# Four-head layer of a graph attention stack: the first group of three neighbours added by VectorE, head by head, in place of TensorE

## The chip, the core and the metric

One core of a Trainium2 chip. The kernel is a single launch that computes four layers; its time is device microseconds of that core, given as the median of several runs. TensorE (PE) does matrix products into PSUM; VectorE (DVE), ScalarE (ACT) and GpSimd (POOL) work along the columns of 128 partitions; SyncE (SP) and POOL issue the DMAs. POOL's indirect DMAs gather table rows by index.

## The reference

Four layers of graph attention with a residual. x is 3327 x 512, adj a 3327 x 3327 matrix of 0 and 1 with some 16 ones in a row. A layer, cut to what matters (layer 1, the second, with four heads of 128 columns):

```
h  = max(layernorm(x), 0)
Wh = (h @ W).reshape(n, 4, 128)
sl, sr = (Wh * a_l).sum(-1), (Wh * a_r).sum(-1)
e  = leaky_relu(sl[i] + sr[j], 0.2), -inf where adj[i, j] == 0
x  = x + elu(sum_j softmax_j(e)[i, j, head] * Wh[j, head])
```

The layers have 8, 4, 1 and 8 heads. What the change touches is the last line's sum over j: a weighted sum of the neighbours' rows, with one weight per neighbour and head, divided at the end by the sum of the weights.

## The kernel before, in words

A first stage (up to about 310 us) turns adj into lists of neighbours, sorted by length. The 26 tiles of 128 rows each then have a fixed number of neighbours, `CAPS`: tile 0 has 36, tile 1 has 25, tile 2 has 23, down to 11 for tile 25. A layer works through its tiles from 25 downward. In layer 1 tiles 25 to 1 go by lists (class `Tile`) and tile 0 is computed densely beside them (class `Several`, spread over the layer's steps).

A list tile is cut into groups of four neighbours (`GROUP`), and a group is a step. `fetch` brings the group's table rows into one of seven buffers g (L865 the tile's own row by SP, L834 the neighbours by POOL's gathers). `scored` computes the group's weights: z on VectorE (L887, L889), then the exponential on ScalarE (L890) into `wt`, a slice of a PSUM tile pw. `group` multiplies the rows by the weights and sums them:

- with one head (layer 2) VectorE does all of it: one `scalar_tensor_tensor` per neighbour over 512 columns, accumulating in PSUM (L909, L911);
- with more heads VectorE multiplies each neighbour's 512 columns by the weights, broadcast over each head's columns (L918). The tile's first neighbour goes straight into the PSUM bank `po`, the others into a buffer m (three of them, four neighbours each), and TensorE adds every m row to the bank by a matmul with the identity (L923). In fp32 each such matmul is two MATMULs in the profile.

When a tile's last group is done, `divisors` (L929 to L931) and, two steps on, `means` (L941) divide the bank; then come the ELU (`bent`, L947 and L949 on ScalarE; L955 on VectorE), the residual (L961), the layer norm for the next layer (L969, L972 on ScalarE; L977, L438, L440 on VectorE), four transposes and sixteen projection MATMULs (`project`, L468), and the scaled row (`rows`, L475 on ScalarE), which SP writes to the next layer's table (L995).

The dense tile 0 takes in every few steps: two loads by SP (L1250, L1251), weights on ScalarE (L1261, L1262, L1267), scaled features (L1278, L1279), the mask on VectorE (L1283) and products on TensorE (L1301).

The order on all engines but SP is written out by hand (`manual_schedule`): each engine runs its instructions in the order in which the program issues them. Step s issues its fetches (7 ahead), the pieces put at "first" (the dense tile's mask and products, transposes), the scores of step s + 1, the pieces put at "scored", the group of step s, and the pieces at "last" (divisors, means, the residual, the projection).

Of the kernel before, what the change touches and what calls it, by code (L numbers as in the profile page):

```python
# [15 lines left out]
OP = mybir.AluOpType  # L16
AX = mybir.AxisListType

P = 128
# [3 lines left out]
HEADS = [8, 4, 1, 8]  # L23
# [11 lines left out]
ROW = 528  # L35
# [488 lines left out]
def tile_gat_stack(ctx: ExitStack, tc: tile.TileContext, x, adj, adjT, ws, avs, out):  # L524
# [266 lines left out]
    with cond.Else():  # L791
        tile_gat_lists(tc, x, adj, ws, avs, out, ident, half, slots, L, low, spare, tabx, tabs)
# [3 lines left out]
def tile_gat_lists(ctx: ExitStack, tc: tile.TileContext, x, adj, ws, avs, out, ident, half, slots, L, low, spare, tabx, tabs):  # L796
# [7 lines left out]
    nc = tc.nc  # L804
    NP, F = x.shape
# [39 lines left out]
    class Tile:  # L845
# [51 lines left out]
        def group(self, i):  # L897


            H, K, wt = HEADS[self.l], CAPS[self.t], self.wt  # L900
            D = F // H
            k0, n, g = self.groups[i]
            if H == 1:
                for q in range(n):
                    v = g[:, q, :].rearrange("p (s m) -> p s m", s=2)[:, :, :F // 2]
                    acc = self.po.rearrange("p (s m) -> p s m", s=2)
                    w = wt[:, k0 + q, 0:1]
                    if k0 + q == 0:
                        nc.vector.tensor_scalar(acc, v, w, None, OP.mult)  # L909
                    else:  # L910
                        nc.vector.scalar_tensor_tensor(acc, v, w, acc, OP.mult, OP.add)  # L911
                return
            m = pools["m"].tile([P, GROUP, F], F32, name="m")
            for q in range(n):
                v = g[:, q, :].rearrange("p (s m) -> p s m", s=2)[:, :, :F // 2]

                out_ = self.po if k0 + q == 0 else m[:, q, :]
                nc.vector.tensor_tensor(out_.rearrange("p (s h d) -> p s h d", s=2, d=D),  # L918
                                        v.rearrange("p s (h d) -> p s h d", d=D),
                                        wt[:, k0 + q, :H].rearrange("p (s h) -> p s h", s=2)  # L920
                                        .unsqueeze(3).to_broadcast([P, 2, H // 2, D]), OP.mult)
            for q in range(k0 == 0, n):
                nc.tensor.matmul(self.po, ident, m[:, q, :], start=False, stop=(k0 + q == K - 1),  # L923
                                 skip_group_check=True)

        def divisors(self):
            H, K = HEADS[self.l], CAPS[self.t]
            den = self.den = small.tile([P, 8], F32, name="den")
            nc.vector.tensor_reduce(den[:, :H], self.wt[:, :K, :H].rearrange("p k h -> p h k"), AX.X, OP.add)  # L929
            nc.vector.tensor_scalar_max(den[:, :H], den[:, :H], TINY)  # L930
            nc.vector.reciprocal(den[:, :H], den[:, :H])  # L931
# [420 lines left out]
    for l in range(NL):  # L1352
# [3 lines left out]
        with ExitStack() as c2:  # L1356
# [44 lines left out]
            for s in range(-1, at_end):  # L1401
# [10 lines left out]
                if 0 <= s < len(steps):  # L1412
                    tl, i = steps[s]
# [55 lines left out]
```

## Time and profile before

| | |
|---|---|
| runs of the kernel before | 3008.34 us median of 3 (2991.2 to 3010.58) |
| span of the profiled execution, first to last instruction | 2971.7 us (its own time around the span is not given) |
| busy: TensorE, VectorE, ScalarE, POOL | 2211.9, 1923.1, 934.6, 1731.4 us |
| the four layers in the span | 315 to 1106, 1106 to 1850, 1850 to 2311, 2311 to 2972 us |
| L923, sums on TensorE, the whole kernel | 2414 MATMULs; 812 of them in layer 1 |
| L918, products on VectorE | 1207 into m and 74 into the bank; 406 and 25 of them in layer 1 |

Busy times of TensorE are modelled and overlap: a MATMUL of 512 fp32 columns lasts 0.59 us in the records and the next starts 0.43 us after it. The clock column of the windows view is TensorE's mean granted clock; TensorE's clock is seen to halve now and then, and MATMULs then start 0.85 us apart.

### The profile page before, as it was taken

To read this page: it belongs to the slowest core of one execution; us is meant where nothing else is said; L and a number is where in the kernel's file an instruction comes from. 1 tells how busy PE (TensorE), PEld (TensorE's weight loads), DVE (VectorE), ACT (ScalarE), POOL (GpSimd) and SP (SyncE) were. 2 spreads that over 40 slices of the span, in tenths; PEclk is the share of its full clock that TensorE was granted. 3 is DMA by queue.
4 is the path that set the end of the run, shared out by engine and by line. 5 is a ranking of instruction groups with operands and counts; after the bars stand their busy time and mean duration, and the time that the engine had idled before them with its cause. 6 is when DMAs were issued, how large, how long until landed. Compare 5 with 4: busy or idle time off the path is not lost.

```text
span 2971.7 us, 27155 instructions
## 1 busy us (share of the span) xinstructions
PE 2211.9 (74%) x7082; PEld 1246.1 (42%) x7082; DVE 1923.1 (65%) x4968; ACT 934.6 (31%) x2502; POOL 1731.4 (58%) x1717
## 2 busy tenths in 40 slices
PE   4777677776777764767777877588696688878887
PEld 2564233343433332434444444244354454545443
DVE  7987666655565533656665665598888366666665
ACT  5872122322221111322222322244333333323330
POOL 7885455565566635544556562676664556555653
PEclk9988888888898887988888898799898898989888
DMA  6885576786676756755667673787785566656663
GB/s 230 325 291 161 165 228 200 211 254 207 195 225 197 199 130 200 200 157 174 187 190 210 179 209 92 234 255 240 241 246 153 168 193 204 185 170 198 195 189 111
DMA packets 260731, 594.21 MB, mean 200 GB/s; under 512 B 103699, under 2 KB 121107, under 8 KB 256214
## 3 DMA queue, kind: packets, MB, share of 16 engines
q0 software_dynamic: 124368, 432.13, 49.8%
q1 hardware_dynamic: 132454, 153.45, 16.4%
q10 hardware_dynamic: 3744, 6.82, 0.7%
q8 instruction: 57, 0.93, 0.1%
q14 instruction: 108, 0.88, 0.1%
HBM read 542.60 MB, written 49.65 MB: 199 GB/s over the span
## 4 chain that ended last, share of the span: by engine, by line
PE 24%; DVE 18%; issue 14%; another core or an unknown queue 8%; ACT 5%; POOL 3%; DMA 2%; SPq 0%; DVEq 0%; POOLq 0%; ACTq 0%
PE bank L923 16%; DVE m L918 6%; PE pv L468 4%; PE whole L1301 3%; DVE bank L911 3%; POOL g L834 3%; ACT r L1267 1%; DVE z L889 1%; DVE z L887 1%; DVE x L961 1%; PE whole L1153 1%; DMA g<-tab,idxb 1%; DVE em L1126 1%; DVE q L438 1%
## 5 line engine op out<-in xcount | busy, mean ns | idle before, releaser
L923 PE MATMUL bank<-m,ident 128*128 128x512 f32 x2414 | 1232.2, 659 | 335.9 <-DVE m L918 197.3
L918 DVE TENSOR_TENSOR m<-g,pw 128x512 f32<-128x512 f32 x1207 | 752.5, 682 | 384.1 <-ACT pw L890 209.2
L834 POOL DMA_INDIRECT g<-tab,idxb x712 | 678.8, 953 | 482.0 <-issue 197.1
L923 PEld LDWEIGHTS bank<-m,ident 128*128 128x128 f32 x2414 | 488.8, 211 | 942.1 <-issue 582.4
L468 PE MATMUL pv<-w,hT 128*128 128x264 f32 x1664 | 434.9, 416 | 87.8 <-ACT hT L457 61.8
L834 POOL DMA_INDIRECT g<-tabx,twiceb x342 | 324.8, 950 | 230.7 <-issue 147.7
L834 POOL DMA_INDIRECT g<-tab,idxa x297 | 283.7, 955 | 248.4 <-issue 83.9
L468 PEld LDWEIGHTS pv<-w,hT 128*128 128x128 f32 x1664 | 334.1, 205 | 190.3 <-ACT hT L457 68.7
L890 ACT ACTIVATE pw<-z 128x32 f32<-128x32 f32 (+4 forms) x356 | 67.8, 191 | 850.7 <-DVE z L889 484.2
L1153 PE MATMUL whole<-ve,em 128*128 128x512 f32 x468 | 229.4, 642 | 54.1 <-issue 22.9
L1301 PE MATMUL whole<-L,room 128*128 128x130 f32 x1248 | 173.3, 290 | 59.9 <-issue 59.5
L1301 PEld LDWEIGHTS whole<-L,room 128*128 128x128 f32 x1248 | 164.7, 202 | 91.4 <-issue 89.7
L694 POOL TENSOR_TENSOR key<-a,keys 128x3328 int32<-128x3328 int32 (+1 forms) x29 | 189.3, 6530 | 16.3 <-DVE cand L703 11.8
L911 DVE SCALAR_TENSOR_TENSOR bank<-g,L,bank 128x512 f32<-128x512 f32 x243 | 183.3, 754 | 11.1 <-remote 2.0
L1153 PEld LDWEIGHTS whole<-ve,em 128*128 128x128 f32 x468 | 94.0, 206 | 167.4 <-issue 124.5
L834 POOL DMA_INDIRECT g<-tabx,twicea x99 | 94.7, 956 | 104.1 <-issue 51.1
L450 PE MATMUL pt<-ident,xn 128*128 128x128 f32 x416 | 70.8, 298 | 104.7 <-ACT xn L969 60.8
L703 DVE MAX8 cand<-key 128x8 f32<-128x208 int32 x416 | 144.3, 365 | 0.1
L475 ACT ACTIVATE v<-pv,rstd 128x528 f32<-128x528 f32 x78 | 54.2, 694 | 274.4 <-remote 126.5
L1267 ACT ACTIVATE r<-low,L 128x384 f32<-128x384 f32 x208 | 121.2, 583 | 16.9 <-remote 9.5
L918 DVE TENSOR_TENSOR bank<-g,pw 128x512 f32<-128x512 f32 x74 | 51.5, 696 | 100.7 <-ACT pw L890 69.2
L450 PEld LDWEIGHTS pt<-ident,xn 128*128 128x128 f32 x416 | 54.7, 153 | 144.4 <-ACT xn L969 69.1
(180 smaller groups left out, 2195.7 us busy)
## 6 DMA issues: line engine op xcount, KB each, us to landing
a<-in_adj SPq DMA_DIRECT2D x25, 1664.0 KB
tab<-v SPq DMA_DIRECT2D x78, 264.0 KB
ve<-tab SPq DMA_DIRECT2D x78, 264.0 KB
g<-tab SPq DMA_DIRECT2D x65, 264.0 KB
tabx<-vx SPq DMA_DIRECT2D x26, 528.0 KB
g<-tab,idxb POOLq DMA_INDIRECT x712
low<-tab SPq DMA_DIRECT2D x52, 132.0 KB
spare<-tab SPq DMA_DIRECT2D x52, 132.0 KB
```

The source lines that it names most:

```text
L450: nc.tensor.transpose(pt[:, k, :], xn[:, k * P:(k + 1) * P], ident)
L468: nc.tensor.matmul(pv[:, s, :HF + 8], hT[:, k, :], W.w[:, k, s, :], start=(k == 0), stop=(k == KC - 1))
L694: nc.gpsimd.tensor_tensor(key[:, c:c + quarter], a[:, c:c + quarter], keys[:, c:c + quarter], OP.mult)
L703: nc.vector.max(cand[:, g * 8:(g + 1) * 8], key[:, g * SEG:(g + 1) * SEG])
L834: nc.gpsimd.indirect_dma_start(out=out_, out_offset=None, in_=table, in_offset=bass.IndirectOffsetOnAxis(ap=which, axis=0))
L890: nc.scalar.activation(self.wt[:, k0:k0 + n, :H], z, AF.Exp)
L911: nc.vector.scalar_tensor_tensor(acc, v, w, acc, OP.mult, OP.add)
L918: nc.vector.tensor_tensor(out_.rearrange("p (s h d) -> p s h d", s=2, d=D), v.rearrange("p s (h d) -> p s h d", d=D), wt[:, k0 + q, :H].re ...
L923: nc.tensor.matmul(self.po, ident, m[:, q, :], start=False, stop=(k0 + q == K - 1), skip_group_check=True)
L1153: nc.tensor.matmul(tl.po.rearrange("p (s m) -> p s m", s=2), e[:, q * P:(q + 1) * P], v.rearrange("p (s m) -> p s m", s=2)[:, :, :F // 2], ...
L1267: nc.scalar.activation(self.r[:, h, :], self.a[:, g, :], AF.Relu, bias=-1.0, scale=self.b[:, j, g:g + 1])
L1301: nc.tensor.matmul(dst, e[:, h, q * P:(q + 1) * P], mov, start=False, stop=(j == NT - 1), skip_group_check=True)
```

## The change

For the layer with four heads, `group` hands a tile's first group (i == 0) to a new function. VectorE multiplies the first neighbour into the bank as before; the other neighbours of that group, three in every tile, are not multiplied into m and summed by TensorE, but added into the bank by VectorE with one `scalar_tensor_tensor` per neighbour and head, on 128 columns, with the head's weight as the per-partition scalar. From the second group on everything is as it was. The other layers, and tile 0 in this layer, don't run the new code.

```diff
@@ def group(self, i) @@
+            if H == 4 and i == 0:
+                self.headwise(g, n)
+                return
             m = pools["m"].tile([P, GROUP, F], F32, name="m")
             for q in range(n):
@@ class Tile @@
+        def headwise(self, g, n):
+            H = HEADS[self.l]
+            D = F // H
+            v = g[:, 0, :].rearrange("p (s m) -> p s m", s=2)[:, :, :F // 2]
+            nc.vector.tensor_tensor(self.po.rearrange("p (s h d) -> p s h d", s=2, d=D),
+                                    v.rearrange("p s (h d) -> p s h d", d=D),
+                                    self.wt[:, 0, :H].rearrange("p (s h) -> p s h", s=2)
+                                    .unsqueeze(3).to_broadcast([P, 2, H // 2, D]), OP.mult)
+            for q in range(1, n):
+                for h in range(H):
+                    c0 = h * D + h // (H // 2) * (ROW // 2 - F // 2)
+                    acc = self.po[:, h * D:(h + 1) * D]
+                    nc.vector.scalar_tensor_tensor(acc, g[:, q, c0:c0 + D], self.wt[:, q, h:h + 1], acc, OP.mult, OP.add)
```

## The prediction

> **What bounds the kernel now.** Only tiles of the second layer (H is 4 there) run the new code, so I first ask for that layer's share of the span. The windows view, cut at the four layers' list stages (315, 1106, 1850, 2311 us), gives for the second:
>
> ```profile
> 315.00:1106.00 791.00, 573.32 (x1623) 288.25 (x1621) 454.58 (x1200) 176.09 (x467) 455.33 (x479) 0.87 0.70 205
> 1106.00:1850.00 744.00, 559.03 (x1569) 298.15 (x1570) 448.17 (x1209) 202.42 (x614) 385.12 (x406) 0.86 0.62 179
> ```
>
> 744 us, and no engine is full: PE 559 (modelled, overlapping), VectorE 448, POOL 385. So I read what was waited for in that stretch, then the chain over its middle part:
>
> ```profile
> ACT pw L890 <- DVE z L889: 173.5, 60, 13.3
> PEld bank L923 <- DVE m L918: 131.4, 81, 11.4
> ...
> PE bank L923 <- DVE m L918: 97.6, 23, 10.3
> DVE ve L977 <- ACT waste L972: 60.5, 15, 11.3
> ...
> ACT v L475 <- PE bank L923: 39.4, 6, 9.9
> ```
> ```profile
> by line: PE bank L923 33.0%; issue 19.8%; DVE m L918 12.1%; another core or an unknown queue 9.2%; PE pv L468 6.2%; PE whole L1301 2.7%; DVE x L961 1.7%; DVE bank L955 1.7%; ACT pw L890 1.2%; DVE q L438 1.1%; ACT low L1278 1.1%; PE pt L450
> ```
>
> The work goes round: PE clears its queue, ScalarE (L475, L1278, L972) resumes, VectorE finishes the last tile and opens the next, PE starts again. PE is the longest part of the round (33% here), VectorE's products the next (12%). The timeline shows a round's start in a tile of 15 neighbours, and one in a tile of 18:
>
> ```profile
> 1303.56 0.70 DVE L918 TENSOR_TENSOR bank<-g,pw 128x512 f32<-128x512 f32 x1 [0.25 <-ACT pw L890]
> 1304.16 1.88 DVE L918 TENSOR_TENSOR m<-g,pw 128x512 f32<-128x512 f32 x3
> ...
> 1304.90 8.43 PE L923 MATMUL bank<-m,ident 128*128 128x512 f32 x12 [4.68 <-DVE m L918]
> ...
> 1306.97 2.48 DVE L918 TENSOR_TENSOR m<-g,pw 128x512 f32<-128x512 f32 x4 [0.31 <-PE bank L923]
> 1307.10 0.78 ACT L1267 ACTIVATE r<-low 128x128 f32<-128x128 f32 x2
> ...
> 1307.81 0.68 ACT L1278 ACTIVATE low<-low 128x128 f32<-128x128 f32 x2
> ```
> ```profile
> 1496.43 2.84 PE L923 MATMUL bank<-m,ident 128*128 128x512 f32 x6 [1.22 <-DVE bank L918]
> ...
> 1498.12 2.48 DVE L918 TENSOR_TENSOR m<-g,pw 128x512 f32<-128x512 f32 x4 [0.25 <-issue]
> ...
> 1499.11 3.72 PE L468 MATMUL pv<-w,hT 128*128 128x264 f32 x16
> ```
>
> In the first, PE had been idle 4.68 us and starts cold: the six MATMULs of the first group take 5.28 us (1304.90 to 1310.18) where six at full clock take 2.57 (0.43 from start to start). In the second they run warm, with the projection (3.56 us) behind them.
>
> **Removed.** Per tile three products into m (L918) and three sums on TensorE, each two MATMULs at 0.43: 2.57 us of PE, 64 us over 25 tiles. On VectorE four products take 1.88 + 0.60 = 2.4 us. The m tile that is saved is worth nothing: VectorE waited on PE in front of an L918 for 1.6 us in the whole layer. No DMA and no ScalarE instruction changes, and the scores (L887 to L890) keep their place.
>
> **Added.** One product and twelve scalar_tensor_tensor of 128x128, accumulator in PSUM. No row shows that. The nearest, from the third layer and from the sorting, in VectorE's timeline:
>
> ```profile
> 1913.52 3.12 DVE L911 SCALAR_TENSOR_TENSOR bank<-g,L,bank 128x512 f32<-128x512 f32 x4
> ```
> ```profile
> 263.45 6.80 DVE L777 TENSOR_SCALAR low<-fixed,lo 128x128 f32<-128x128 f32 x26
> ```
>
> L911 is the same instruction on 512 columns, each waiting for the one in front: (3.12 - 0.755)/3 = 0.788 apart. The price of a column follows from L1283 (1746 ns at 1536, 414 at 256): 1.04 ns. At 128 columns that makes 0.788 - 0.400 = 0.388 us. L777 is 128 columns out of PSUM with a pointer scalar and waits for nothing: (6.80 - 0.341)/25 = 0.258. So twelve cost 3.1 to 4.7 us, and with the first product, which they await (0.73), less the old 2.4, **VectorE's extra is 1.4 to 3.0 us per tile**, 36 to 75 in the layer. Four heads are four separate slices, so the low price needs that a write to one slice of a bank doesn't hold up the next. The two L1267 write two slices of one PSUM tile and start 0.78 - 0.37 = 0.41 apart; the two L1278, as long (0.387), write SBUF and start 0.30 apart. In PSUM the second waited for the first. I take 3.0. A scalar that is read out of PSUM (here it is; in L911 it lies in SBUF) has no row; the broadcast operand of L918 comes from the same PSUM tile and costs nothing visible, so nothing is added.
>
> The Trainium skill's page "VectorE: DVE Perf Modes" (The DRAIN you can't avoid) says that a semaphore after each VectorE operation costs nothing extra, as the pipe is emptied anyway. By it the price would be 0.26 and the extra 1.4. The rows differ here: behind the last of those four L911 (start 1915.88) the unrelated L929 starts at 1916.55, 0.67 later, where a waiting L911 takes 0.788.
>
> **What of it is on the path.** The second group's first product now starts 3.0 later, and PE can take it 0.74 after that (the shortest trail the trace shows). Before, PE reached the second group later than VectorE's first product of it by a trail, read off the timeline for tiles 25 down to 1: 4.1, 0.7, 0.7, 0.7, 1.0, 0.7, 2.2, 3.2, 3.0, 3.2, 3.1, 1.4, 6.5, 3.7, 5.0, 4.2, 5.0, 5.0, 4.2, 5.0, 4.2, 4.8, 5.6, 3.7, 1.1. A tile changes by 3.73 less its trail, and gains at most 2.57.
>
> - Tiles 13 to 2: PE is behind, the extra is hidden under its queue. The sum is -11.8; for tiles 3 and 2 POOL's gathers are the chain (1738 to 1798 us, one each 1.25 us), which keeps 1.9 of it: -9.9.
> - Tiles 19 to 15: +3.9. PE still starts cold, now in the second group, which in the trace ran warm: the surcharge of 5.2 - 2.6 = 2.6 us stays in each, 13.0. In two of them (17, 16) a landing, not PE, ended the next wait, some 3 us after PE was done; that covers 6.4. Together +10.5.
> - Tiles 23, 21, 14, 1: PE has no backlog, 3.0 + 2.7 + 2.3 + 2.7 = +10.6. PE then idles 2.57 + 2.7, about 5 us, more than the 4.7 behind which it ran cold: 0 to 2.6 for each, I take half, +5.2.
> - Tiles 24, 22, 20: VectorE itself sat idle 5 to 13 us in front of the second group; the extra goes into that. Tile 25 is followed by a 13 us wait. 0.
>
> What is queued behind the twelve on VectorE is L1283 (SP's next mask load, L1251, waits for it) and the next scores, hence ScalarE's L890, and the release of the gather buffer, hence POOL: POOL stands idle 10.30 us in front of its gather at 1306.31, which follows the first group's last product, so it starts 3 us later and has its burst done 10 us before it is next let on.
>
> **Sum:** -9.9 + 10.5 + 10.6 + 5.2 = **+16 us**. The page gives the profiled execution's span, 2971.7 us, and no time around it; the fastest run shown (2991.2) is 19.5 above it. I add the sum to the median, 3008.3: **3024 us**, with 3011 to 3031 as this case's own bounds (no cold second group, or one in every tile of the second and third entry). One per cent is 30 us, about what a measurement of this kernel can tell from no change.
>
> **Rivals.**
>
> *Cheap steps.* The twelve don't wait for each other: extra 1.4. Tiles 13 to 2 then give -26.9 (POOL keeps 4.1 of it), 19 to 15 -3.8 + 13.0 less the 4 that landings cover, the four without backlog +4.5: about -13, 2995 us. For it: m's slices at L918 are written 0.60 apart, without a wait. Against: L1267. Chance 0.13.
>
> *The clock, slower.* In tiles 13 to 2 PE finishes the projection and stands idle until the second group, 2.57 less the gain: 0 to 2.6 us. If that is enough to bring back half clock, ten more tiles pay 2.6, the four without backlog pay in full (5.2), and tiles 17 and 16 aren't covered (6.4): 16 + 26 + 5 + 6, 3062 us. It decides where PE's idle stretch ahead of the second group grows past some 3 us; such stretches of 4.2 to 4.7 us did bring it. For it: the layer's mean granted clock is 0.86 already. Against: idle stretches of 1.2 us (1495 us) left it warm. VectorE becoming the bound is the far end of the same thing: 75 us, 3083. Chance 0.31.
>
> The skill's page "TensorE: Matmul & The Clock Gate" (Part 1: The HAM clock gate) puts the return to half clock behind an idle window of about 3.4 us that runs freely; by it the 2.6 us would mostly stay warm and this rival would shrink to the +16.
>
> *PE's time comes back.* PE sets the whole round, 33% of the chain against 12%: two thirds of the 64 us, 2965 us. Against: VectorE's products feed that same queue. Chance 0.09.
>
> **How the numbers follow.** Forecast 0.47 and cheap steps 0.13 lie within 1%: 0.60. Slower 0.31, faster 0.09. The range runs from 2980 (below the cheap case, above PE's full return) to 3063 (the clock case, without its far end).
>
> **What would show it.** The twelve at 0.39 from start to start, or at 0.26, settles the price. L923 falls from 2414 to 2264 MATMULs. In the layer's window VectorE's busy time rises by some 60 us; PE's falls by about 80, as the modelled durations overlap. Right: PE's waits on VectorE grow, and the layer takes 744 + 16. Wrong: the layer's granted clock falls below 0.83, the steps wait for something else (the PSUM scalar), or ScalarE's waits on PE (L475, L1278) vanish and the layer shortens.

## The result, and the profile after

The changed kernel takes 3017.49 us (median of 20 runs, 2993.67 to 3035.44) where the kernel before, run beside it, takes 3003.74 us (20 runs, 2991.2 to 3026.24). The ratio is **1.0045, 95% interval 1.0026 to 1.0064**: 13.7 us longer, between 8 and 19. The forecast was 16 us longer, within 1%.

The page of the changed kernel (busy time and number of instructions of each engine; then the costliest groups, with the idle time ahead of them and what ended most of it):

```profile
span 3033.7 us, 27055 instructions
...
PE 2167.6 (71%) x6932; PEld 1224.7 (40%) x6932; DVE 1988.3 (66%) x5193; ACT 931.4 (31%) x2502; POOL 1728.3 (57%) x1717
...
L926 PE MATMUL bank<-m,ident 128*128 128x512 f32 x2264 | 1164.9, 661 | 386.7 <-DVE m L921 269.9
```

L926 (the old L923) has the 2264 MATMULs that were foretold, 150 fewer. TensorE's busy time falls by only 44 us, VectorE's rises by 65. This execution took 3035.44 us, 18 more than the median. Some of its length has nothing to do with the change: its first layer, which doesn't run the new code, ended 27 us later than in the profile before. And the profile before is of a short execution: a run's time is 1.7 to 2.1 us above its span in every run here that has both, so the span of 2971.7 us stands for some 2973, below the shortest of the 20 runs (2991.2). The layer's own length, from its first MATMUL to the next layer's first product, is 755.1 us before and 776.3 after, one profile each. The windows view of that stretch after (length; busy time of PE, PEld, DVE, ACT and POOL with the instruction counts; granted clock, DMA share, GB/s):

```profile
1138.80:1915.10 776.30, 503.85 (x1416) 272.02 (x1415) 510.67 (x1433) 204.85 (x628) 393.45 (x416) 0.83 0.60 176
```

The same stretch before has 557.70 for PE, 448.39 for VectorE and a granted clock of 0.86. VectorE now works longer than TensorE here. The waits in this layer after:

```profile
ACT pw L890 <- DVE z L889: 210.1, 56, 13.2
...
PEld bank L926 <- DVE m L921: 165.7, 82, 10.9
PE bank L926 <- DVE m L921: 156.2, 35, 19.8
...
POOL g L834 <- DVE bank L943: 94.6, 11, 14.6
```

PE's waits on VectorE's products were 97.6 us in 23 places; they are 156.2 in 35. The chain over the layer's middle, from tile 14's first product on (1449 to 1738 us; the prediction's was 1411 to 1700 us), shows the same from the other side (shares of the stretch):

```profile
by line: another core or an unknown queue 20.6%; issue 19.2%; DVE m L921 14.9%; DVE bank L943 14.3%; PE bank L926 3.5%; ACT pw L890 2.5%; DVE bank L935 2.4%; DVE q L438 2.4%; ACT low L1297 2.1%; DVE x L980 1.9%; DVE bank L974 1.8%; ACT wast
```

TensorE's sums were a third of that chain and are 3.5%. VectorE's new steps, L943, have 14.3% now. The largest entry, "another core or an unknown queue", rose from 9.2% to 20.6%; the last section says what these waits are. The timeline of tile 18 (15 neighbours), the same tile as the first one that the prediction shows:

```profile
1330.94 0.70 DVE L935 TENSOR_TENSOR bank<-g,pw 128x512 f32<-128x512 f32 x1 [0.25 <-ACT pw L890]
1331.67 4.71 DVE L943 SCALAR_TENSOR_TENSOR bank<-g,pw,bank 128x128 f32<-128x128 f32 x12
...
1336.65 0.94 POOL L834 DMA_INDIRECT g<-tab,idxb  x1 [14.26 <-DVE bank L943]
...
1337.31 2.48 DVE L921 TENSOR_TENSOR m<-g,pw 128x512 f32<-128x512 f32 x4 [0.31 <-ACT pw L890]
...
1338.05 3.75 PE L926 MATMUL bank<-m,ident 128*128 128x512 f32 x4 [10.43 <-DVE m L921]
```

Twelve steps in 4.71 us, the last as long as one alone (0.36): (4.71 - 0.36)/11 = 0.395 us from start to start. From the bank's product to the second group's first product 6.37 us pass where 3.41 did. PE, which used to start 1.3 us after the bank's product, starts 7.1 us after it, after 10.43 us of idleness, and cold: from the second on, its MATMULs begin 0.85 us apart.

### The profile page after: what moved, and what is told of

Its sections match the earlier page's. It is cut to its first block, busy times and chain, and to the rows that moved or that the text cites. A ratio compares the mean times of both kernels' runs of the same rounds, so it can differ in the third digit from the quotient of the medians.

```text
span 3033.7 us, 27055 instructions
## 1 busy us (share of the span) xinstructions
PE 2167.6 (71%) x6932; PEld 1224.7 (40%) x6932; DVE 1988.3 (66%) x5193; ACT 931.4 (31%) x2502; POOL 1728.3 (57%) x1717
## 3 DMA queue, kind: packets, MB, share of 16 engines
q1 hardware_dynamic: 132454, 153.45, 15.8%
## 4 chain that ended last, share of the span: by engine, by line
DVE 23%; PE 18%; issue 13%; another core or an unknown queue 10%; ACT 6%; POOL 2%; DMA 2%; DVEq 0%; SPq 0%; ACTq 0%; POOLq 0%
PE bank L926 10%; DVE m L921 7%; PE pv L468 4%; DVE bank L943 3%; DVE bank L911 3%; PE whole L1320 3%; POOL g L834 2%; PE whole L1172 1%; ACT r L1286 1%; DVE z L889 1%; DVE x L980 1%; DVE z L887 1%; ACT pw L890 1%; DVE q L438 1%
## 5 line engine op out<-in xcount | busy, mean ns | idle before, releaser
L926 PE MATMUL bank<-m,ident 128*128 128x512 f32 x2264 | 1164.9, 661 | 386.7 <-DVE m L921 269.9
L921 DVE TENSOR_TENSOR m<-g,pw 128x512 f32<-128x512 f32 x1132 | 705.0, 681 | 388.8 <-ACT pw L890 265.3
L926 PEld LDWEIGHTS bank<-m,ident 128*128 128x128 f32 x2264 | 456.3, 211 | 963.4 <-issue 541.7
L468 PE MATMUL pv<-w,hT 128*128 128x264 f32 x1664 | 454.4, 429 | 131.5 <-ACT hT L457 96.4
L468 PEld LDWEIGHTS pv<-w,hT 128*128 128x128 f32 x1664 | 347.5, 213 | 242.3 <-ACT hT L457 106.4
L457 ACT ACTIVATE hT<-pt 128x512 f32<-128x512 f32 x104 | 61.4, 590 | 247.1 <-remote 202.7
L943 DVE SCALAR_TENSOR_TENSOR bank<-g,pw,bank 128x128 f32<-128x128 f32 x300 | 108.0, 360 | 17.7 <-DVE bank L943 6.6
```

What stands on the lines that cost most here:

```text
L468: nc.tensor.matmul(pv[:, s, :HF + 8], hT[:, k, :], W.w[:, k, s, :], start=(k == 0), stop=(k == KC - 1))
L943: nc.vector.scalar_tensor_tensor(acc, g[:, q, c0:c0 + D], self.wt[:, q, h:h + 1], acc, OP.mult, OP.add)
```

## The experiments

The runs fell on chips of two speeds. On the slower (here A) ran the predicted pair and the first four kernels; the kernel before takes 3003.74 us there beside the changed kernel and 3017.31 us beside the four (median of 35 runs). On the quicker (here B) ran the others; the kernel before takes 2430 us. Each ratio is against the kernel before on the same chip, and ratios are compared within one speed.

### Which tiles lose (chip A)

The guard in `group` of the changed kernel, first for the tiles in which the prediction saw a gain, then for the others:

```diff
-            if H == 4 and i == 0:
+            if H == 4 and i == 0 and 2 <= self.t <= 13:
```
```diff
-            if H == 4 and i == 0:
+            if H == 4 and i == 0 and not 2 <= self.t <= 13:
```

> The head-wise first group only in tiles 2 to 13, where PE trailed VectorE by 3.7 to 6.5 us before; the other 13 tiles as before. The account of the prediction says PE's backlog hides VectorE's extra 3.0 us there and 9.9 us are gained: about 10 us below the kernel before (ratio 0.997). The rival, read off the changed kernel's trace, where PE trails by only 0.74 us in these tiles too and their stretch takes 379 us after 374: no gain, 0 to +6 us (1.000 to 1.002).

> The head-wise first group only in tiles 14 to 25 and 1, where PE had little or no backlog; tiles 2 to 13 as before. The prediction's account: all of the loss is here, +26 us (1.009). The rival: the loss is here but smaller, +8 to +14 us (1.003 to 1.005), since tiles 2 to 13 gain nothing.

Measured: tiles 2 to 13 alone 3014.92 us, ratio 1.0001 [0.9971, 1.0032]; the others alone 3026.32 us, ratio 1.0042 [1.0012, 1.0073], 12.7 us. By these figures the loss of 13.7 lies in the second set, and the first set brings nothing: the predicted gain of 9.9 us there is just outside the interval (9.9/3017 is 0.0033, the interval reaches 0.0029 below 1). The two intervals overlap, so a part of the loss may lie in the first set.

### The two halves, each alone (chip A)

TensorE's relief alone: the first group's sums left out.

```diff
-            for q in range(k0 == 0, n):
+            for q in range(n if H == 4 and i == 0 else k0 == 0, n):
                 nc.tensor.matmul(self.po, ident, m[:, q, :], start=False, stop=(k0 + q == K - 1),
```

> TensorE's part alone: VectorE multiplies the first group's neighbours into m as before, and TensorE doesn't add them (neighbours 2 to 4 of each tile of the four-head layer are left out of the sum). 2.57 us of PE less per tile, 64 in all, and nothing more on VectorE. The account: PE can gain no more than its trail behind VectorE; 25 to 30 us less (0.990 to 0.992), as the cold start moves to the second group in tiles 15 to 19. A rival in which PE alone sets the layer: 43 to 64 us less (0.979 to 0.986).

VectorE's extra alone: all sums as before, and four chained operations on 512 columns behind the first group's products, into a slice of m that the first group doesn't use.

```diff
+            if H == 4 and i == 0:
+                for q in range(4):
+                    nc.vector.tensor_tensor(m[:, 0, :], m[:, 0 if q else 1, :], g[:, q, :F], OP.max)
```

> VectorE's part alone: products into m and all sums on TensorE as before, and behind the first group's products four more operations on VectorE that write an unused part of m, each waiting for the one in front, some 2.9 us per tile, 73 in all. The account: hidden where PE trails by more than 3.7 us, so +10 to +15 us (1.003 to 1.005). The rival in which VectorE's chain sets the layer: +40 to +73 us (1.013 to 1.024).

Measured: the relief alone 2994.74 us, ratio 0.9914 [0.9883, 0.9946], a gain of 26 us, as expected. The extra alone 3015.67 us, ratio 0.9994 [0.9964, 1.0024]: nothing, where 10 to 15 us had been expected. Its extra is nearly that of the change, 6.20 us from the bank's product to the second group's first product in tile 18, which begins at 1322.10, where the change has 6.37. By these runs 2.8 us more of VectorE per tile cost between -11 and +7 us on this chip, in a kernel where PE has the first group's six MATMULs to do meanwhile.

The halves don't add up: -26 and 0 make -26, the change measures +14. One thing that neither half holds is that in the change PE has *no* work of the tile's sums until VectorE's steps and the second group's first product are over.

The profiles, one each, tell where the halves differ from the change. From the first product of one tile to that of another pass, in us:

| | tiles 19 to 15 | tiles 13 to 2 |
|---|---|---|
| without the new code (kernel before; the tiles that the first experiment left as they were) | 135.8, 137.6 | 373.9, 373.0 |
| with it (changed kernel; the tiles that the first experiment changed) | 149.6, 150.3 | 379.3, 386.5 |
| relief alone | 135.0 | 363.4 |
| extra alone | 139.9 | 382.9 |

In tiles 19 to 15 neither half costs much and both together cost 12 to 15 us. In tiles 13 to 2 it is otherwise: the extra alone takes as long as the change, though TensorE has all its sums there. That the runs of the extra alone show no loss in the whole kernel doesn't fit this well; its profiled execution was 12.7 us above their median.

### Where the extra stands, and how cold PE is (chip B)

To separate these, the same four operations were put between the bank's product and the group's other products, so that PE starts late though it has all its work:

```diff
             for q in range(n):
...
+                if H == 4 and i == 0 and q == 1:
+                    for j in range(4):
+                        nc.vector.tensor_tensor(m[:, 0, :], m[:, 0, :] if j else g[:, 1, :F], g[:, j, :F], OP.max)
```

And in the changed kernel, ten products with zeros on an unused part of the dense tile's bank behind the new group, as soon as its scores are there, in tiles 14 to 25 and 1, meant to keep PE's clock from being taken down before the second group:

```diff
+            if i == 0:
+                self.z0 = z
...
             if H == 4 and i == 0:
                 self.headwise(g, n)
+                if self.t >= 14 or self.t == 1:
+                    self.warm()
...
+        def warm(self):
+            po = getattr(wholes, "po", None)
+            if po is not None:
+                for _ in range(10):
+                    nc.tensor.matmul(po[0][:, 258:512], zero.to_broadcast([P, P]),
+                                     self.z0[:, 0, 0:1].to_broadcast([P, 254]), start=False, stop=False,
+                                     skip_group_check=True)
```

> The same extra VectorE work as in the run of VectorE's part alone (some 2.9 us per tile, all sums on TensorE), but between the tile's first product and the other three, so that TensorE gets its first row 2.9 us later. VectorE's and TensorE's work are the same as in that run, which took no time. If what counts is when TensorE first gets work in a tile: +30 to +73 us (1.010 to 1.024). If VectorE's total counts: as that run, 0.998 to 1.002.

> The changed kernel, and in tiles 14 to 25 and 1 TensorE is given 20 small MATMULs of zeros (254 columns into unused columns of the dense tile's bank) while VectorE works through the head-wise group, so that it is running when the second group's first product arrives. It adds PE work and takes no wait away. If the loss comes from a cold start in the second group (2.6 us in eight to ten tiles): 13 to 25 us less than the changed kernel, ratio to before 0.996 to 1.000. If the clock isn't the cause: as the changed kernel or a little slower, 1.004 to 1.006.

Measured: extra ahead of the products 2507.74 us, ratio 1.0329 [1.0311, 1.0347]; kept warm 2491.56 us, ratio 1.026 [1.0243, 1.0276]. Both are far more than anything on chip A and more than had been expected of them, and the changed kernel had not run on B. So four kernels were then run together on one chip of speed B: the changed kernel itself, the extra alone, and these two again.

> The changed kernel itself, beside the other three on the same chip. The kernel before has been seen at some 3010 us on one chip and at 2430 us on another; ratios are compared within one chip only. Where the kernel before takes some 3010 us: 1.0045 as measured, +14 us. Where it takes some 2430 us and the long waits that hid VectorE's extra are missing: theory of VectorE's extra, 25 tiles at 3.0 us less what PE's relief gives back, +45 to +75 us (1.019 to 1.031).

> VectorE's part alone again: four more operations behind the first group's products, 2.8 us a tile (the bank to the second group's first product took 6.20 us where it took 3.41), all sums on TensorE. At 3010 us: 0.9994 as before. At 2430 us: if TensorE's start in a tile counts, less than half of the changed kernel's loss, since TensorE has the first group's sums to do in that time (1.005 to 1.012); if VectorE's total counts, as the changed kernel or above it (1.025 to 1.035).

> The same VectorE work between the tile's first product and the other three: TensorE gets its first row 2.9 us later. At 2430 us it gave 1.033, +80 us, the whole of 25 times 2.9 us. At 3010 us: +25 to +73 us (1.008 to 1.024) if TensorE's start in a tile counts; 0.997 to 1.003, as VectorE's part alone, if it is only the amount of VectorE work.

> The changed kernel with TensorE kept running by zeros through the head-wise group of tiles 14 to 25 and 1. At 3010 us: if the loss is the cold start of the second group, 13 to 25 us less than the changed kernel (0.996 to 1.000); if not, 1.004 to 1.006. At 2430 us it gave 1.026: the changed kernel without the zeros comes out above that (1.03) if the cold start counts, below it (1.019 to 1.025) if not.

| beside a kernel before of 2431.18 us | median, us | ratio [95%] |
|---|---|---|
| extra alone, behind the products | 2483.43 | 1.0222 [1.0203, 1.0242] |
| the change, kept warm | 2488.39 | 1.025 [1.0229, 1.0272] |
| the change | 2496.45 | 1.0279 [1.0259, 1.0299] |
| extra alone, ahead of the products | 2508.14 | 1.0323 [1.0303, 1.0343] |

The windows view of the middle of the layer on B, for the changed kernel and for the extra alone:

```profile
930.00:1530.00 600.00, 464.54 (x1365) 251.81 (x1364) 504.81 (x1412) 196.03 (x605) 383.85 (x405) 0.89 0.74 218
```
```profile
930.00:1530.00 600.00, 508.88 (x1534) 272.74 (x1535) 512.86 (x1302) 198.65 (x611) 385.12 (x402) 0.96 0.74 217
```

Here VectorE is busy 505 to 513 of 600 us; on A it is 511 of 776. The extra alone, free on A, costs 2.2% on B, 54 us or 2.2 of its 2.8 us per tile, between the two expectations and nearer to the one in which VectorE's total counts. On the quicker chip most of VectorE's extra is on the path.

The first and the last row of the table are the same instructions on every engine, and differ only in whether PE gets its first group before the extra or after it. That place alone costs 1%, some 25 us or 1.0 us per tile. The timelines of tile 18 show where PE starts. Extra alone, behind the products:

```profile
1073.84 0.70 DVE L918 TENSOR_TENSOR bank<-g,pw 128x512 f32<-128x512 f32 x1 [0.25 <-ACT pw L890]
1074.44 1.88 DVE L918 TENSOR_TENSOR m<-g,pw 128x512 f32<-128x512 f32 x3
...
1075.17 2.84 PE L926 MATMUL bank<-m,ident 128*128 128x512 f32 x6 [1.30 <-DVE m L918]
...
1076.23 2.86 DVE L924 TENSOR_TENSOR m<-m,g 128x512 f32<-128x512 f32 x4
...
1080.03 2.48 DVE L918 TENSOR_TENSOR m<-g,pw 128x512 f32<-128x512 f32 x4 [0.31 <-ACT pw L890]
```

Extra alone, ahead of the products:

```profile
1076.93 0.70 DVE L921 TENSOR_TENSOR bank<-g,pw 128x512 f32<-128x512 f32 x1 [0.25 <-ACT pw L890]
...
1078.25 2.14 DVE L919 TENSOR_TENSOR m<-m,g 128x512 f32<-128x512 f32 x3
...
1081.04 9.27 PE L926 MATMUL bank<-m,ident 128*128 128x512 f32 x14 [3.38 <-DVE m L921]
```

The change on the same chip:

```profile
1081.02 0.70 DVE L935 TENSOR_TENSOR bank<-g,pw 128x512 f32<-128x512 f32 x1 [0.25 <-ACT pw L890]
...
1081.75 4.72 DVE L943 SCALAR_TENSOR_TENSOR bank<-g,pw,bank 128x128 f32<-128x128 f32 x12
...
1087.40 2.48 DVE L921 TENSOR_TENSOR m<-g,pw 128x512 f32<-128x512 f32 x4 [0.31 <-ACT pw L890]
...
1088.14 4.63 PE L926 MATMUL bank<-m,ident 128*128 128x512 f32 x5 [6.31 <-DVE m L921]
```

In the first, PE starts 1.33 us after the bank's product and does the first group's six MATMULs in 2.84 us, warm, under VectorE's extra. In the second it starts 4.11 us after it. In the change it starts 7.12 us after it, from 6.31 us of idleness, and five MATMULs take 4.63 us. Against the extra ahead of the products the change has 64 us less for PE to do and is about 11 us quicker, though its extra is some 4 us longer (2.96 against 2.79 us per tile, 25 x 0.17); so PE's relief is worth some 15 us there. Against the extra behind them it has the same relief and is still 13 us slower, 4 of them its longer extra.

But the 25 us can't be carried over to the change. They arise in tiles 13 to 5, where PE, with all its sums to do after a late start, falls behind: from tile 13's first product to tile 4's pass 217.6 us with the extra behind the products, 235.6 with it ahead of them, and 219.0 in the change, no more over the first than its longer extra. The 13 us between the change and the extra behind the products are, in these two profiles, 4.2 before the layer's first product, where both run the same code, and 7.6 from tile 25's first product to tile 1's. So a late start is shown to cost time where PE still has its sums; of the change's loss on B it can be a few us.

The change with the zeros has a ratio of 1.025 against 1.0279 without them (intervals that overlap slightly; 8 us of medians). The granted clock in the same window rises from 0.89 to 0.94. The zeros did only a part of what they were meant to: tile 25 got none, and in tiles 23, 21, 20, 18, 16 and 14 the second group began cold all the same (in tile 18, 4.48 us after the last zeros), so that only those of tiles 24, 22, 19, 17, 15 and 1 began warm. Of those, tiles 24, 22, 19, 17 and 15 took 0.7 us less together than in the change. So on B the cold start is a small part of the change's loss of 68 us (0.0279 x 2431).

### What a step costs (chip B)

The accumulator of the first group moved out of PSUM into SBUF; only the last neighbour's four steps write the bank:

```diff
+            acc = pools["m"].tile([P, GROUP, F], F32, name="m")[:, 0, :]
...
-                    acc = self.po[:, h * D:(h + 1) * D]
-                    nc.vector.scalar_tensor_tensor(acc, g[:, q, c0:c0 + D], self.wt[:, q, h:h + 1], acc, OP.mult, OP.add)
+                    hs = slice(h * D, (h + 1) * D)
+                    out_ = self.po[:, hs] if q == n - 1 else acc[:, hs]
+                    nc.vector.scalar_tensor_tensor(out_, g[:, q, c0:c0 + D], self.wt[:, q, h:h + 1], acc[:, hs], OP.mult, OP.add)
```

> The changed kernel with the first product and eight of the twelve steps accumulated in SBUF (an unused part of m), and only the last neighbour's four steps written to the bank. Theory of the price: steps on separate SBUF slices don't wait for one another, 0.26 us apart instead of 0.39, VectorE's extra 1.9 us instead of 3.0 per tile, and the start of the second group some 1.1 us earlier: about 10 to 20 us less than the changed kernel, ratio to before 0.998 to 1.001. Rival, the waits don't matter or remain in SBUF: 1.004 as the changed kernel.

Measured: 2470.16 us, ratio 1.0174 [1.0159, 1.0189], against 1.0279 for the change (on another chip of the same speed). VectorE's timeline in tile 18:

```profile
1071.37 0.69 DVE L936 TENSOR_TENSOR m<-g,pw 128x512 f32<-128x512 f32 x1 [0.25 <-ACT pw L890]
1072.10 2.22 DVE L945 SCALAR_TENSOR_TENSOR m<-g,pw,m 128x128 f32<-128x128 f32 x8
1074.24 1.56 DVE L945 SCALAR_TENSOR_TENSOR bank<-g,pw,m 128x128 f32<-128x128 f32 x4
...
1076.72 2.48 DVE L921 TENSOR_TENSOR m<-g,pw 128x512 f32<-128x512 f32 x4 [0.31 <-ACT pw L890]
```

Eight steps into SBUF: (2.22 - 0.35)/7 = 0.267 us apart. Four into slices of the PSUM bank: (1.56 - 0.36)/3 = 0.40 apart, though none of the four reads what another wrote. The scalar lies in PSUM in both. The trace's records of the instructions show why: each step into the bank waits on VectorE's own semaphore, which the step in front raises, and starts 0.036 us after that one's end. Of the eight steps into m the second to fourth carry no such wait; the last four carry one, and start without delay all the same. So the program, as it was built, puts a wait between two writes to the bank, and a separate slice doesn't help; between separate slices of m it puts none that delays a step. Whether the chip itself would hold up the second write isn't shown. The extra falls from 2.96 to 1.94 us per tile (1076.72 - 1071.37 - 3.41), 25 us in 25 tiles, and the time falls by 26: on this chip the extra counts one for one.

### A version meant to beat both (chip B)

The first group left to TensorE, so that PE starts early; instead, in the second and third group VectorE adds the products in pairs, and TensorE sums two rows where it summed four:

```diff
+            qs = list(range(k0 == 0, n))
+            if H == 4 and i in (1, 2) and n == 4:
+                for q in (0, 2):
+                    nc.vector.tensor_tensor(m[:, q, :], m[:, q, :], m[:, q + 1, :], OP.add)
+                qs = [0, 2]
-            for q in range(k0 == 0, n):
+            for q in qs:
...
```

> A version after the findings: the first group as in the kernel before, so that TensorE starts early; in the second and third groups VectorE adds the products in pairs in m (two additions of 512 columns each group, some 0.6 to 0.7 us each), and TensorE sums two rows instead of four: 3.4 us of PE less per tile, some 2.5 us more on VectorE, behind TensorE's trail. If PE relief behind an early start is worth what leaving the first group's sums out was worth (26 us for 64 us of PE), and VectorE's extra is free there: 20 to 35 us less than before, 0.988 to 0.993. Rival, the additions hold up the second group's sums as the head-wise steps did: 1.00 to 1.01.

Measured: 2474.2 us, ratio 1.0174 [1.0154, 1.0194], worse than both the expectation and its rival. On B every kernel that was run with more work on VectorE loses. This one was not run on A, so whether it would gain there stays open. But for the kernel that leaves sums out, nothing that was run beats the kernel before.

## Why the prediction was right, and where it was not

**What is added: right.** The price was given as 0.388 us apart if the steps wait for each other and 0.258 if not. Measured are 0.395 in PSUM and 0.267 in SBUF, so both ends were real prices and the choice, read off the two L1267, was the right one. The extra is 2.96 us per tile (3.0 predicted), and a scalar out of PSUM adds no more than 0.01 us, as assumed. The cheap rival's price is not that of this kernel but that of its variant in SBUF. The prediction cites the Trainium skill's page "VectorE: DVE Perf Modes" (The DRAIN you can't avoid) for a semaphore behind each operation being free. In these runs that holds for a wait that has already been met (the last four steps into m, 0.267 apart like the ones without a wait), but a wait for the operation just in front costs about 0.13 us, 0.395 against 0.267.

**Tiles 13 to 2: wrong, and the step is "PE is behind, the extra is hidden under its queue", -9.9.** Alone they measure 0 by the runs, and in the profiles they take 5 to 14 us longer with the new code (the table above). The first half of the working held: after, PE's trail is 0.74 us in 21 of the 25 tiles, and in tile 11 PE starts the second group 6.72 us after the tile's first product instead of 8.03, 1.3 us earlier as worked out. But the working took it that a tile ends earlier by as much as its second group starts earlier, and it doesn't: tile 11 took 0.8 us less, tiles 10 and 8 took 3.0 and 4.9 more. The extra isn't hidden by PE's queue either: with the extra alone PE still trails by 0.9 to 5.2 us in these tiles, and tiles 8 and 3 take 33.6 and 36.2 us, as in the change (33.4 and 36.2; before, 28.6 and 31.8). PE's saving ends in waiting: in ten of these twelve tiles PE stood idle ahead of the second group, 0.4 to 4.3 us. By which wait the extra reaches the tile's end isn't shown.

**Tiles 19 to 15: +10.5 predicted.** From tile 19's first product to tile 14's pass 149.6 us where 135.8 did, 13.8 more; in the second kernel of the first experiment 150.3, and in the first, where these tiles are as before, 137.6. What the trace shows is as told: PE idles 6.0 to 10.4 us ahead of the second group, and its first MATMULs there last 1.22 us instead of 0.59. The halves fit the account: with the relief alone these second groups begin cold too, and 135.0 us says that 2.57 us less work and the cold start about cancel; with the extra alone they begin warm, at 0.59 to 0.88 us, and it takes 139.9. No run on A keeps PE warm in the change, so the surcharge by itself isn't measured there.

**Tiles without backlog, and the cold surcharge on them, +15.8; tiles 24, 22, 20 and 25 nothing.** From tile 25's to tile 19's first product pass 142.5 us where 145.9 did, so tiles 23 and 21 show no loss. Tile 14 lost 2.1 (23.2 to 25.3 us to the next tile), and from tile 1's first product to the next layer's 3.7 more passed. So this term was too big, half or more of it. Together the tiles outside 13 to 2 were put at +26 and cost 12.7 (+4 to +22 by the interval).

**The sum: +16 against +13.7** is luck: two errors of opposite sign cancelled, a gain of 10 that wasn't there and a loss 13 us too big.

**The clock rival: its mechanism showed, its price didn't.** PE does idle longer ahead of the second group and starts cold in nearly all of tiles 25 to 14. But in tiles 13 to 2 only two of twelve ran the second group cold: tile 12, after 4.33 us of idleness, from the first MATMUL, and tile 13, after 2.99 us, from the second; after 0.4 to 2.7 us the first MATMUL lasted 0.70 and the next ones 0.59. The granted clock in the layer is 0.83, on the bound that the prediction had set for this rival. On B, zeros that keep the clock up in about half of their tiles go with 8 us less; the rival had put 37 (26 + 5 + 6) on the cold starts.

**PE's time comes back: not in the change.** The relief alone brings 26 us on A, not the 43 of that rival, and the change loses it.

**Signs.** VectorE's busy time rose by 62 us in the layer (some 60 foretold), PE's fell by 54 there, not 80: each cold MATMUL counts for longer in the records, 1.06 us against 0.59. PE's waits on VectorE grew, as foretold.

**What stays open.** On A the extra alone is free by its runs and on B it costs 2.2%. In the changed kernel 31.8 us pass from tile 18's first product to the next tile's on A, and 23.5 on B; what holds A back was not settled. How the missing 40 us on A (from -26 to +14) come about is shown in part: in tiles 19 to 15 only both halves together cost much, which fits a late and cold start, and in tiles 13 to 2 the extra alone takes as long as the change, so that a late start explains nothing there. Both rest on single profiles. On A nothing was run that puts the extra ahead of the products.

## What to carry to other kernels

When a change takes work off the engine that is behind, its backlog goes too, and an earlier start of its next piece is not yet a shorter round: follow the work that was added on the other engine to the end of the round, tile by tile. Work that the second engine starts on is a doubtful choice, since that engine then stands idle until the first is done, and the first needs time to spare in any case. On B, where VectorE had little, each us added on it cost 0.8 to 1 us, and 64 us less on TensorE brought 15 at most. Small accumulating steps on VectorE were cheaper into slices of an SBUF tile than into slices of one PSUM bank, where each waited for the one in front.

## What the runs showed of the hardware that was not expected

The same kernel took 3017 us on one chip and 2430 on another, 24% apart, and the same change 0.45% and 2.8%. On A the waits view, over the stretch from 300 to 2400 us of the kernel before, names waits for another core or an unknown queue, in a program on one core:

```profile
ACT v L475 <- remote: 126.5, 11, 19.8
...
ACT hT L457 <- remote: 60.1, 5, 25.8
```

In the profiles of the changed kernel and of the extra alone on B there is no such entry. The name misleads: of the 77 such waits in the whole kernel before, 63 (366 of 500 us), L457's among them, are for nothing but semaphores that TensorE, VectorE or ScalarE instructions of this core raise. The other 14, most of L475's among them, are for a DMA's landing as well, and A's profiles lack most landings (the changed kernel's profile holds 12904 on A and 35463 on B). The clearest case is VectorE waiting only for its own semaphore, raised by the instruction in front: on A it started more than 0.5 us late 15 times in the kernel before (25 us in all, up to 4.0) and 38 times in the changed kernel (65 us), on B never (0.20 us at most). A's profiles also lack raises of TensorE's semaphore, 1533 of 1879 in the changed kernel where B's has all, so that shares of A's waits and chains are rough. What makes these waits end late, whether they are the difference between the chips, and whether they hide VectorE's extra on A was not tested.

A write to one 128-column slice of a PSUM bank was followed by a write to another slice 0.40 us later, against 0.267 in SBUF; in this program that is a semaphore wait for the write in front. And idleness of one length did not always end the same way. In the changed kernel the clock halved 0.86 us before the second group's start behind 4.33 us of idleness (tile 12) and 0.48 us after it behind 2.99 us (tile 13); in the kernel with the new code in tiles 2 to 13 alone it halved 0.70 us after the start behind 4.69 us (tile 12), whose first MATMUL still lasted 0.70. In these traces the clock changes only between full and half, and apart from the last stretch of a trace it keeps either for a multiple of 3.41 us.
